# More bands of two 3x3 convolutions in the mixed form, with the statistics of their outputs taken by accumulators

## The chip, the cores and the metric

The kernel runs on one core of a Trainium2 chip, as one launch. The metric is the device time of a run in microseconds; lower is better. Five engines work side by side, each through its own queue in order: TensorE (PE) multiplies, VectorE (DVE) and ScalarE (ACT) do elementwise work, GpSimd (POOL) does small fills and issues some DMAs, SyncE (SP) issues the other DMAs. They wait for each other by semaphores.

## The reference

Two layers on x of shape (4, 128, 64, 64), fp32. The first is group norm, 4-head attention over the 4096 pixels of an image, a projection and a residual. The second is what the change is about:

```python
def conv3x3_decomposed(x, wq):
    xp = jnp.pad(x, ((0, 0), (0, 0), (1, 1), (1, 1)))
    out = jnp.zeros((B, wq.shape[0], H, W), dtype=x.dtype)
    for kh in range(3):
        for kw in range(3):
            out = out + jnp.einsum('bchw,oc->bohw', xp[:, :, kh:kh + H, kw:kw + W], wq[:, :, kh, kw])
    return out
...
residual = x
out = conv3x3_decomposed(x, lsq_quantize(w1, alpha1))
out = jax.nn.relu(batchnorm(out, gamma1, beta1))
out = conv3x3_decomposed(out, lsq_quantize(w2, alpha2))
out = batchnorm(out, gamma2, beta2)
out = jax.nn.relu(out + residual)
```

`batchnorm` takes the mean and variance of a channel over all images and pixels, so a convolution has to be finished before its normalization is known, and the second convolution cannot begin before that.

## The kernel before

Attention comes first: 32 blocks of 512 queries, in an order of the queues that is written out by hand. It leaves its result `y0` in device memory, one image of 128 x 4096 each. The change does not touch it, apart from the last of its side tasks, which load and split the first bands.

Each convolution (`layer(i, prepare, done)`) goes through 16 bands, four of 16 rows in each image. Bands are numbered m = 0 to 15, band 3 being the last of image 0; `bandlist` holds them. There are two ways to compute a band.

- Plain (`conv`, L814): the input is split into a rounded part `hi` and the remainder `lo`, and two halves of 8 rows are summed in PSUM over 9 taps and the two parts: 2 x 18 = 36 matmuls of 128x512. Evacuation: for each half, DVE takes statistics from PSUM (BN_STATS, L928), then ACT copies it to `cv` (L929).
- Mixed (`conv_by_two`, L860): rows go in pairs. DVE forms a difference of rows two apart (`vo`, L594) and the sum and difference of neighbouring rows (`vi`, L596 and L597); ACT rounds both (`uo`, `ui`, L605) and DVE takes the remainders (`lo`, `li`, L607). The four products need 3 taps times two parts each: 24 matmuls of 128x512, with `wmix` made from the weights by `mix_weights`. `rows_of_two` puts even and odd rows together: ACT copies one product to the odd rows (L868), DVE does two inner additions (L869, L870), which need the first PSUM tile, and two outer ones (L871, L872), which need the second. DVE then takes the statistics from `cv` (L919).

Which bands are mixed is `BY_TWO`, one set for each convolution. Band 15 is always plain and stands by itself at the end of `layer`; after it ten idle matmuls (`keep_warm`) bridge `batch_norm`.

PSUM has a pool `pss` of three tiles, two banks each, for plain bands and the first pair of a mixed band, and a pool `psa` of two single banks. The second pair of a mixed band lies alternately in two tiles of `psa` (named x and y) or in one tile of `pss` (named z).

Inputs are prepared two bands ahead: `prepare(m)` (`first` or `second`) stands in program order between the matmuls of band m and its evacuation, and prepares band m+2. In the first convolution it loads band m+3 from `y0` (`load_band`) and splits band m+2 (`split_band`); at m=5 `count_bad` tests a bound of the attention by a 1x1 matmul (`nbad`), which stands on PE behind band 5; at m=14 the weights of the second convolution are mixed. In the second convolution `relu_band` normalizes band m+2 on ACT (L974, L985) and prepares it in one go; `load_res` fetches the quarter images of `y0` for the residual. Band inputs share nine buffers of `kpool` (`stack_tile`); further parts of mixed bands lie in `upper`.

The end adds the residual on DVE (L1038), applies ReLU on ACT (L1039) and stores 16 quarter images from the queues of SP and ACT.

Of the kernel before, what the change touches and what calls it, by code (L numbers as in the profile page):

```python
# [16 lines left out]
F32 = mybir.dt.float32  # L17
AF = mybir.ActivationFunctionType
ALU = mybir.AluOpType
# [59 lines left out]
def _fast_body(ctx, tc, x, norm_w, norm_b, qkv_wt, qkv_b, proj_wt, proj_b,  # L79
# [144 lines left out]
    def stack_tile(name):  # L224
        return kpool.tile([P, KW], F32R, name=name, tag="k")

    def f32(t):
        return t.bitcast(F32)
# [340 lines left out]

    def split(t, name, beside=True):  # L570

        hi, lo = band_tile(f"hi{name}"), band_tile(f"lo{name}")
        if beside:
            nc.vector.tensor_copy(hi, f32(t))
        else:
            nc.scalar.copy(hi, f32(t))
        nc.vector.tensor_tensor(lo, f32(t), f32(hi), ALU.subtract)
        return hi, lo
# [6 lines left out]

    BY_TWO = (set((4, 6, 8, 10, 12, 14)), set((2, 4, 6, 8, 10, 12, 14)))

    def mixed(t, name):


        t = f32(t)
        outer, inner = (stack_tile(f"{n}{name}")[:, : BR * PW].rearrange("p (r w) -> p r w", w=PW)
                        for n in ("vo", "vi"))
        nc.vector.tensor_tensor(f32(outer), t[:, 0:BR, :], t[:, 2 : BR + 2, :], ALU.subtract)  # L594
        odd, even = t[:, 1 : BR + 1 : 2, :], t[:, 2 : BR + 2 : 2, :]
        nc.vector.tensor_tensor(f32(inner)[:, : BR // 2, :], odd, even, ALU.add)  # L596
        nc.vector.tensor_tensor(f32(inner)[:, BR // 2 :, :], even, odd, ALU.subtract)  # L597
        def part(n):
            if n == "uo":
                return stack_tile(f"{n}{name}")[:, : BR * PW].rearrange("p (r w) -> p r w", w=PW)  # L600
            return upper.tile([P, BR, PW], F32R, name=f"{n}{name}", tag="u")

        hi, lo = ([part(n + k) for k in "oi"] for n in "ul")
        for u, v in zip(hi, (outer, inner)):
            nc.scalar.copy(u, f32(v))  # L605
        for u, v, w in zip(hi, (outer, inner), lo):
            nc.vector.tensor_tensor(w, f32(v), f32(u), ALU.subtract)  # L607
        return [(o[:, 0::2, :], i[:, : BR // 2, :], i[:, BR // 2 :, :], o[:, 1::2, :])
                for o, i in (hi, lo)]

# [5 lines left out]
    def split_band(b, g):  # L616
        m = bandlist.index((b, g))
        way = mixed if m in BY_TWO[0] else lambda t, name: split(t, name, m < 3)
        ready[0, b, g] = way(raw[b, g], f"0_{b}_{g}")

# [219 lines left out]
    wq.append(mid.tile([P, TAPS, P], F32R, name="wq1"))  # L840
    upper = ctx.enter_context(tc.tile_pool(name="upper", bufs=6))
    wmix = mid.tile([P, 2, 3, P], F32R, name="wmix")
# [20 lines left out]

    def rows_of_two(a, c, y):

        even, odd = (y.rearrange("p (r e w) -> p r e w", e=2, w=W)[:, :, e, :] for e in range(2))
        a0, a1, c0, c1 = (u.rearrange("p (r w) -> p r w", w=W) for u in (*a, *c))
        nc.scalar.copy(odd, a1)  # L868
        nc.vector.tensor_tensor(even, odd, a0, ALU.add)  # L869
        nc.vector.tensor_tensor(odd, a0, odd, ALU.subtract)  # L870
        nc.vector.tensor_tensor(even, even, c0, ALU.add)  # L871
        nc.vector.tensor_tensor(odd, odd, c1, ALU.subtract)  # L872

# [25 lines left out]
    def layer(i, prepare, done):  # L899


        st = mid.tile([P, B * NB, 6], F32, name=f"st{i}")
        end = mid.tile([P, 15], F32, name=f"end{i}")
        nc.gpsimd.memset(end[:, 0:1], float((B * NB - 2) * FB))
        for m, (b, g) in enumerate(bandlist[:-1]):
            if m in BY_TWO[i]:
                a = conv_tile(i, b, g)
                a = [a[:, j, :] for j in range(2)]
                if (max(BY_TWO[i]) - m) % 4:
                    c = [psa.tile([P, FB], F32, name=f"c{i}_{b}_{g}{j}", tag="a") for j in "xy"]  # L910
                else:
                    c = pss.tile([P, 2, FB], F32, name=f"c{i}_{b}_{g}z", tag="s")
                    c = [c[:, j, :] for j in range(2)]
                conv_by_two(ready[i, b, g], a, c, i)
                prepare(m)
                y = cv[b][:, 2 * g * FB : (2 * g + 2) * FB]
                rows_of_two(a, c, y)
                for j in range(2):
                    nc.vector.bn_stats(st[:, b * NB + 2 * g + j, :], y[:, j * FB : (j + 1) * FB])  # L919
                continue  # L920
            ps = done[m] if m < len(done) else conv_tile(i, b, g)
            for j in range(2):
                if m >= len(done):
                    conv(ready[i, b, g], ps[:, j, :], j, wq[i])
            prepare(m)
            for j in range(2):
                c = 2 * g + j
                nc.vector.bn_stats(st[:, b * NB + c, :], ps[:, j, :])  # L928
                nc.scalar.copy(cv[b][:, c * FB : (c + 1) * FB], ps[:, j, :])  # L929
        nc.vector.bn_aggr(end[:, 1:3], st.rearrange("p j s -> p (j s)")[:, : 6 * B * NB - 12])  # L930
        nc.vector.tensor_scalar(end[:, 2:3], end[:, 2:3], float((B * NB - 2) * FB), None, ALU.mult)
        b, g = bandlist[-1]
        for j in range(2):
            ps = psa.tile([P, FB], F32, name=f"c{i}_last{j}", tag="a")
            conv(ready[i, b, g], ps, j, wq[i])
            c = 2 * g + j
            nc.vector.bn_stats(end[:, 3 + 6 * j : 9 + 6 * j], ps)
            nc.scalar.copy(cv[b][:, c * FB : (c + 1) * FB], ps)
        prepare(len(bandlist) - 1)
        keep_warm(10)  # L940
        return batch_norm(i, end)

    def count_bad():
# [7 lines left out]
        nc.vector.tensor_copy(cnt, nbad[0:1, 0:1])  # L951

    def first(m):
        if m == 5:
            count_bad()
        if m == 5:
            raw["w"] = f32(stack_tile("raw_w"))[:, : TAPS * P].rearrange("p (t o) -> p t o", o=P)
            nc.sync.dma_start(out=raw["w"], in_=wqd)
        if m == 6:
            nc.vector.tensor_copy(wq[1], raw["w"])  # L960
        if m == 14:
            mix_weights(1)
        if 0 < m < len(bandlist) - 3:
            load_band(*bandlist[m + 3])
        if m + 2 < len(bandlist) and m > 0:
            split_band(*bandlist[m + 2])

    a1, c1 = layer(0, first, early)

    def relu_rows(b, g, t, r0, r1):  # L970

        inner, lo, hi = t["inner"]
        a, e = max(r0 + g * BR - 1, lo), min(r1 + g * BR - 1, hi)
        nc.scalar.activation(inner[:, a - lo : e - lo, :],  # L974
                             cv[b].rearrange("p (h w) -> p h w", w=W)[:, a:e, :], AF.Relu,
                             bias=c1, scale=a1)
        nc.scalar.copy(t["hi"][:, r0:r1, :], f32(t["t"])[:, r0:r1, :])
        nc.vector.tensor_tensor(t["lo"][:, r0:r1, :], f32(t["t"])[:, r0:r1, :],
                                f32(t["hi"])[:, r0:r1, :], ALU.subtract)

    def relu_band(b, g, pieces=((0, BR + 2),)):
        if bandlist.index((b, g)) in BY_TWO[1]:
            t = band_tile(f"t1_{b}_{g}")
            inner, lo, hi = border(t, g)
            nc.scalar.activation(inner, cv[b].rearrange("p (h w) -> p h w", w=W)[:, lo:hi, :],  # L985
                                 AF.Relu, bias=c1, scale=a1)
            ready[1, b, g] = mixed(t, f"1_{b}_{g}")
            return
        t = {n: band_tile(f"{n}1_{b}_{g}") for n in ("t", "hi", "lo")}
        t["inner"] = border(t["t"], g)  # L990
        for r0, r1 in pieces:
            relu_rows(b, g, t, r0, r1)
        ready[1, b, g] = t["hi"], t["lo"]

# [13 lines left out]
    ready[1, b0, g0] = t["hi"], t["lo"]  # L1008
    relu_band(*bandlist[1])

# [4 lines left out]
    def load_res(b, i):  # L1015
        if b < B - 1:
            t = mid.tile([P, HN], F32, name=f"res{b}_{i}")
        else:
            t = f32(stack_tile(f"res{b}_{i}"))[:, :HN]
        res[b, i] = t  # L1020
        nc.sync.dma_start(out=t, in_=y0[b][:, i * HN : (i + 1) * HN])

    def second(m):
        if m + 2 < len(bandlist):
            relu_band(*bandlist[m + 2])
        if m < 4 * B - 4:
            load_res(m // 4, m % 4)

    a2, c2 = layer(1, second, [])
    for i in range(4):  # L1030
        load_res(B - 1, i)
    for b in range(B):
# [468 lines left out]
```

## Time and profile before

| what | value |
|---|---|
| median of 3 runs | 2512.17 us (2512.08 to 2512.52) |
| profiled execution, first to last instruction | 2511.1 us |
| PE busy | 2471.6 us, 98% of the span |
| DVE busy | 2194.6 us, 87% |
| ACT busy | 2123.7 us, 85% |
| statistics of the first convolution merged (`bmv`, L887) | at 2359.94 us |
| statistics of the second convolution merged | at 2481.11 us |

The three runs are times of whole executions; the profiled execution is a further one, of which the page gives the span. The profile gives each instruction of that one execution with start, duration and what it waited for. "L814" is a line of the kernel; `c<-hi,wq` is an instruction's output and inputs. In a row of groups the count, the busy time and the mean duration come first, then the idle time of the engine just before these instructions and what ended it. In a row of the timeline the start and the duration are in us, and a bracket at the end tells how long the engine had been idle and whom it waited for. A row of windows gives, for a stretch of the execution, its length, the busy time and number of instructions of each engine, the granted TensorE clock, the DMA share and the DMA rate.

### The profile page before, as it was taken

The page shows a single profiled execution, that of the slowest core. Times are in us where ns is not written, and L with a number is a line of the kernel's source. Part 1 is how long each engine was busy: PE and PEld are TensorE (multiplying, and loading weights), DVE is VectorE, ACT ScalarE, POOL GpSimd, SP SyncE. Part 2 cuts the span into 40 slices and gives each one's busy share as a digit, 9 for nine tenths or more (in the row PEclk, how much of TensorE's full clock was granted, in tenths as well). Part 3 has the DMA queues.
Part 4 walks back from the last instruction along what each step waited for, and adds up shares of the span by engine and source line. Part 5 has one row for each costly group of instructions (what it writes and reads, how often), then busy time and mean ns, then how long its engine had stood idle before and what let it go on. Part 6 is the DMA issues. An engine that isn't in the chain of part 4 may idle for free.

```text
span 2511.1 us, 64860 instructions
## 1 busy us (share of the span) xinstructions
PE 2471.6 (98%) x28552; PEld 1473.1 (59%) x28552; DVE 2194.6 (87%) x1486; ACT 2123.7 (85%) x2306; POOL 281.6 (11%) x461
## 2 busy tenths in 40 slices
PE   9999999999999999999999999999999999999995
PEld 6555555555555555555555555555555555567774
DVE  6899888899988988889988888889999999978686
ACT  5999888999988889999989889989999999954354
POOL 2111111111011111111011111110001010010000
PEclk9999999999999999999999999999999999999998
DMA  6877667788766676787757676797666666664204
GB/s 198 191 181 169 169 176 173 171 200 187 181 155 165 175 170 155 167 207 183 172 143 191 167 156 161 169 217 178 141 143 144 143 133 150 142 135 93 110 1 169
DMA packets 148954, 403.85 MB, mean 161 GB/s; under 512 B 59416, under 2 KB 60184, under 8 KB 120120
## 3 DMA queue, kind: packets, MB, share of 16 engines
q0 software_dynamic: 45840, 280.39, 48.9%
q1 hardware_dynamic: 100952, 113.60, 17.1%
q10 hardware_dynamic: 1872, 5.64, 0.6%
q8 instruction: 226, 3.70, 0.6%
q14 instruction: 64, 0.52, 0.1%
HBM read 107.48 MB, written 56.42 MB: 65 GB/s over the span
## 4 chain that ended last, share of the span: by engine, by line
PE 89%; issue 4%; DMA 3%; DVE 2%; ACT 1%; POOL 0%; ACTq 0%; SPq 0%; POOLq 0%; DVEq 0%
PE s L442 41%; PE acc L456 37%; PE c L814 3%; DMA rm<-p 3%; PE l L488 1%; PE pq L317 1%; PE c L860 1%; PE po L317 1%; PE pv L317 1%; PE pk L317 1%; DVE r L471 1%; PE c_2z L860 1%; ACT res L1039 0%; ACT p L444 0%; PE c_last L814 0%
## 5 line engine op out<-in xcount | busy, mean ns | idle before, releaser
L444 ACT ACTIVATE p<-s 128x1024 f32<-128x1024 f32 x2048 | 1950.5, 1032 | 201.9 <-PE s L442 154.0
L471 DVE TENSOR_TENSOR r<-r,p 128x2048 f32<-128x2048 f32 x768 | 1757.9, 2289 | 64.4 <-ACT p L444 14.0
L442 PE MATMUL s<-q,k 64*128 64x512 f32 x8192 | 1138.9, 409 | 2.1 <-ACT p L444 2.0
L456 PE MATMUL acc<-p,v 128*32 128x256 f32 x16384 | 1026.4, 383 | 0.0
L442 PEld LDWEIGHTS s<-q,k 64*128 64x128 f32 x8192 | 715.6, 184 | 410.9 <-issue 165.9
L456 PEld LDWEIGHTS acc<-p,v 128*32 128x32 f32 x16384 | 462.4, 109 | 483.7 <-issue 248.5
L466 POOL DMA_DIRECT2D rm<-p x160 | 139.5, 872 | 808.5 <-ACT p L444 602.0
L929 ACT COPY cv<-c 128x512 f32<-128x512 f32 x34 | 19.9, 586 | 101.6 <-DVE st L928 101.6
L352 DVE SCALAR_TENSOR_TENSOR kst<-pk,b,kst 128x512 fp32r<-128x512 f32 x32 | 24.0, 750 | 83.3 <-PE s L442 68.5
L469 DVE TENSOR_TENSOR r<-p,p 128x2048 f32<-128x2048 f32 x32 | 73.2, 2287 | 12.4 <-ACT p L444 10.7
L814 PE MATMUL c<-hi,wq 128*128 128x512 f32 x306 | 79.1, 403 | 1.6 <-ACT hi L1003 1.3
L814 PE MATMUL c<-lo,wq 128*128 128x512 f32 x306 | 78.5, 400 | 0.0
L352 DVE SCALAR_TENSOR_TENSOR qst<-pq,b,qst 128x512 fp32r<-128x512 f32 x32 | 24.0, 751 | 58.5 <-PE s L442 45.5
L814 PEld LDWEIGHTS c<-hi,wq 128*128 128x128 f32 x306 | 57.2, 188 | 19.2 <-issue 2.1
L814 PEld LDWEIGHTS c<-lo,wq 128*128 128x128 f32 x306 | 57.6, 188 | 15.4
L356 POOL DMA_DIRECT2D qd<-qst x31 | 23.6, 760 | 263.0 <-DVE qst L352 221.1
L492 POOL DMA_DIRECT2D r<-rm x31 | 26.2, 844 | 216.7 <-DMA rm<-p 86.9
L928 DVE BATCH_NORM_STATS2 st<-c 128x6 f32<-128x512 f32 x34 | 23.7, 697 | 20.8 <-ACT cv L929 11.2
L356 POOL DMA_DIRECT2D kd<-kst x27 | 20.0, 740 | 174.8 <-DVE kst L352 166.3
L464 POOL DMA_DIRECT2D rm<-p x32 | 17.8, 557 | 177.2 <-ACT p L444 100.6
L488 PE MATMUL l<-r,ones 128*32 128x256 f32 (+1 forms) x504 | 37.7, 382 | 0.0
L351 ACT ACTIVATE kst<-pk,b 128x512 fp32r<-128x512 f32 x32 | 22.3, 699 | 17.3 <-PE pk L317 17.2
(185 smaller groups left out, 1023.9 us busy)
## 6 DMA issues: line engine op xcount, KB each, us to landing
rm<-p POOLq DMA_DIRECT2D x192, 1024.0 KB, 8.0
q<-qd SPq DMA_DIRECT2D x248, 128.0 KB
r<-rm POOLq DMA_DIRECT2D x31, 1024.0 KB, 7.9
x<-in_x_dram SPq DMA_DIRECT2D x86, 256.0 KB
k<-kd SPq DMA_DIRECT2D x124, 128.0 KB
qd<-qst POOLq DMA_DIRECT2D x31, 512.0 KB, 5.1
kd<-kst POOLq DMA_DIRECT2D x27, 512.0 KB, 5.0
y<-x POOLq DMA_DIRECT2D x32, 256.0 KB, 6.4
```

What stands on the lines that cost most here:

```text
L317: nc.tensor.matmul(out[cs, :], w[:, cs], x, start=True, stop=True)
L352: nc.vector.scalar_tensor_tensor(lo, ps[what], bias, t[:, 0, :], ALU.add, ALU.subtract)
L356: (nc.sync if start else nc.gpsimd).dma_start(out=dst[b, j].rearrange("s p n -> p s n"), in_=t)
L442: nc.tensor.matmul(s[:, i, :], k[r, half, c0 : c0 + P], q[r, half, part, :], start=(part == 0), stop=(part == 1))
L444: nc.scalar.activation(pts[step][:, 2 * half : 2 * half + 2, :], s, AF.Exp, scale=SCALE)
L456: nc.tensor.matmul(acc[n][h * D : (h + 1) * D, cs], v[:, kt % KB, h * D : (h + 1) * D], pt[:, h, cs], start=(kt == 0 and half == 0), stop= ...
L466: nc.gpsimd.dma_start(out=msum[n], in_=pt, accum_op=ALU.add)
L469: nc.vector.tensor_tensor(rsum[n], pts[step - 1], pt, ALU.add)
L471: nc.vector.tensor_tensor(rsum[n], rsum[n], pt, ALU.add)
L488: nc.tensor.matmul(t["l"][h * D : (h + 1) * D, cs], ones, r[:, h, cs], start=first, stop=end)
L814: nc.tensor.matmul(ps.rearrange("p (r w) -> p r w", w=W), w[:, tap, :], part[:, r0 + kh : r0 + kh + RB, kw : kw + W], start=(n == 0), stop ...
L860: nc.tensor.matmul(ps.rearrange("p (r w) -> p r w", w=W), w[:, kw, :], part[m][:, :, kw : kw + W], start=(n == 0), stop=(n == 5))
```

## The change

`BY_TWO` grows from 6 + 7 to 9 + 10 bands, so 19 of 32 bands are mixed. `uo` moves to the pool `upper`, which gets 12 buffers instead of 6.

For mixed bands the two BN_STATS go. The two outer additions become SCALAR_TENSOR_TENSOR with an accumulator output, the sum; ACT squares the finished band of 1024 elements with an accumulator output, its bias being minus the mean of band 0 (`shift`). At the end of a layer these sums are merged with the statistics of the plain bands by six small instructions more than before.

Preparation is cut into parts. `begin` forms `vo`, `vi` and the rounded copies, `rest` the remainders, `later` does loads, the count and the ReLU. In a mixed band they are placed between the steps of evacuation: odd copy, `begin`, inner additions, `rest`, `later`, outer additions, square. In plain bands the evacuation comes after all three. In the second convolution ReLU is applied to band m+3, one band before its preparation. Mixing the weights of the second convolution moves behind the preparation of its band 1. The residual of image 2 is loaded, like that of image 3, after the second convolution in program order, into buffers of `upper`.

```diff
-    BY_TWO = (set((4, 6, 8, 10, 12, 14)), set((2, 4, 6, 8, 10, 12, 14)))
+    BY_TWO = (set((3, 4, 6, 7, 9, 10, 12, 13, 14)), set((2, 3, 4, 6, 7, 9, 10, 12, 13, 14)))
...
-    def mixed(t, name):
+    def mixed_parts(t, name):
...
+        def mix():
+            nc.vector.tensor_tensor(outer, t[:, 0:BR, :], t[:, 2 : BR + 2, :], ALU.subtract)
+            odd, even = t[:, 1 : BR + 1 : 2, :], t[:, 2 : BR + 2 : 2, :]
+            nc.vector.tensor_tensor(inner[:, : BR // 2, :], odd, even, ALU.add)
+            nc.vector.tensor_tensor(inner[:, BR // 2 :, :], even, odd, ALU.subtract)
+            for u, v in zip(hi, (outer, inner)):
+                nc.scalar.copy(u, v)
+
+        def rest():
+            for u, v, w in zip(hi, (outer, inner), lo):
+                nc.vector.tensor_tensor(w, v, f32(u), ALU.subtract)
...
-    upper = ctx.enter_context(tc.tile_pool(name="upper", bufs=6))
+    upper = ctx.enter_context(tc.tile_pool(name="upper", bufs=12))
...
-        nc.scalar.copy(odd, a1)
-        nc.vector.tensor_tensor(even, odd, a0, ALU.add)
-        nc.vector.tensor_tensor(odd, a0, odd, ALU.subtract)
-        nc.vector.tensor_tensor(even, even, c0, ALU.add)
-        nc.vector.tensor_tensor(odd, odd, c1, ALU.subtract)
+
+        def copy():
+            nc.scalar.copy(odd, a1)
+
+        def inner():
+            nc.vector.tensor_tensor(even, odd, a0, ALU.add)
+            nc.vector.tensor_tensor(odd, a0, odd, ALU.subtract)
+
+        def outer():
+            nc.vector.scalar_tensor_tensor(even, even, 1.0, c0, ALU.mult, ALU.add,
+                                           accum_out=sums[:, 0:1])
+            nc.vector.scalar_tensor_tensor(odd, odd, 1.0, c1, ALU.mult, ALU.subtract,
+                                           accum_out=sums[:, 1:2])
...
         for m, (b, g) in enumerate(bandlist[:-1]):
+            begin, rest, later = prepare(m)
             if m in BY_TWO[i]:
...
                 conv_by_two(ready[i, b, g], a, c, i)
-                prepare(m)
                 y = cv[b][:, 2 * g * FB : (2 * g + 2) * FB]
-                rows_of_two(a, c, y)
-                for j in range(2):
-                    nc.vector.bn_stats(st[:, b * NB + 2 * g + j, :], y[:, j * FB : (j + 1) * FB])
+                k = two.index(m)
+                copy, inner, outer = rows_of_two(a, c, y, sums[:, 2 * k : 2 * k + 2])
+                copy()
+                begin()
+                inner()
+                rest()
+                later()
+                outer()
+                junk = ready[i, b, g][0][4].rearrange("p r w -> p (r w)")[:, : 2 * FB]
+                nc.scalar.activation(junk, y, AF.Square, bias=shift[:, 1:2],
+                                     accum_out=squares[:, k : k + 1])
                 continue
...
-            prepare(m)
+            begin()
+            rest()
+            later()
...
+            if m == 0:
+                mv = small.tile([P, 2], F32, name=f"first{i}", tag="mv")
+                nc.vector.bn_aggr(mv, st[:, 0:2, :].rearrange("p j s -> p (j s)"))
+                nc.vector.tensor_copy(shift[:, 0:1], mv[:, 0:1])
+                nc.vector.tensor_scalar(shift[:, 1:2], mv[:, 0:1], -1.0, None, ALU.mult)
...
-        if m == 14:
-            mix_weights(1)
...
+    mix_weights(1)
+    relu_band(2)
...
     def second(m):
+        begin = rest = nothing
         if m + 2 < len(bandlist):
-            relu_band(*bandlist[m + 2])
-        if m < 4 * B - 4:
-            load_res(m // 4, m % 4)
+            begin, rest = parts_of(1, m + 2, raw[1, m + 2])
+
+        def later():
+            if m + 3 < len(bandlist):
+                relu_band(m + 3)
+            if m < 4 * B - 8:
+                load_res(m // 4, m % 4)
+
+        return begin, rest, later
```

## Prediction, made before the changed kernel was run

> **What bounds the kernel now.** I read in this order: granted clock and stages, TensorE's own order of time in the convolutions, then the groups of VectorE (DVE) and ScalarE (ACT) there. First the windows by stage: attention; its end; first convolution; second; tail.
>
> ```profile
> core 0: us, PE busy (x) PEld busy (x) DVE busy (x) ACT busy (x) POOL busy (x), PEclk, DMA share, GB/s
> 0.00:2207.00 2207.00, 2198.63 (x27178) 1266.31 (x27182) 1968.65 (x1212) 1986.36 (x2152) 270.10 (x374) 1.00 0.72 169
> 2207.00:2258.00 51.00, 51.00 (x434) 31.86 (x427) 38.97 (x32) 24.21 (x27) 4.93 (x16) 1.00 0.65 136
> 2258.00:2361.00 103.00, 101.66 (x436) 79.87 (x435) 79.82 (x113) 35.25 (x45) 2.63 (x27) 1.00 0.44 123
> 2361.00:2481.00 120.00, 118.71 (x504) 93.68 (x503) 86.85 (x110) 59.47 (x65) 3.43 (x45) 1.00 0.05 18
> 2481.00:2511.10 30.10, 1.57 (x15) 1.38 (x13) 20.31 (x23) 18.43 (x18) 0.55 (x1) 0.59 0.71 281
> ```
>
> The change lies in the third and fourth stretch. PE is full there at clock 1.00, DVE at 72 to 78%. PE waits only twice within the first convolution. Its timeline there:
>
> ```profile
> 2262.90 2.42 PE L814 MATMUL c<-hi,wq 128*128 128x512 f32 x9 [0.32 <-ACT hi L576]
> ...
> 2287.09 0.19 PE L950 MATMUL nbad<-ones,bad 128*1 128x1 f32 x2 [1.02 <-DVE bad L948]
> ```
>
> So matmuls removed here are time saved, as long as DVE and ACT can still prepare the bands. The chain that ended last gives the price: a plain band is "8.60 PE c L814 x36", so 0.239 us a matmul; a mixed band has 24, 5.74 us. What DVE and ACT need for a band (groups of the two convolutions, name, count, busy us, mean ns and idle before; then, with min/median/max ns, the tail's two instructions and the attention's last addition; last the table load):
>
> ```profile
> L928 DVE BATCH_NORM_STATS2 st<-c 128x6 f32<-128x512 f32 x34 | 23.7, 697 | 20.8 <-ACT cv L929 11.2 <-PE c L814 9.6
> L919 DVE BATCH_NORM_STATS2 st<-cv 128x6 f32<-128x512 f32 x26 | 16.7, 686 | 0.5
> L607 DVE TENSOR_TENSOR li<-vi,ui 128x1056 fp32r<-128x1056 f32 x13 | 16.4, 1258 | 0.0
> L594 DVE TENSOR_TENSOR vo<-t 128x1056 f32<-128x1056 f32 x13 | 16.3, 1251 | 11.7 <-ACT t L985 11.7
> L871 DVE TENSOR_TENSOR cv<-cv,c_0x 128x512 f32<-128x512 f32 x6 | 4.1, 676 | 0.0
> ```
>
> ```profile
> L1038 DVE SCALAR_TENSOR_TENSOR res<-cv,ba,res x17: 744/1275/1277, 2482.8 to 2500.8; 128x1024 f32<-128x1024 f32 x15, 128x512 f32<-128x512 f32 x2
> L1039 ACT ACTIVATE res<-res,bc x17: 721/1134/1149, 2483.5 to 2503.7; 128x1024 f32<-128x1024 f32 x15, 128x512 f32<-128x512 f32 x2
> ```
>
> ```profile
> L547 DVE SCALAR_TENSOR_TENSOR x<-po,bp,x x32: 742/746/751, 168.1 to 2253.9; 128x512 f32<-128x512 f32 x32
> ```
>
> ```profile
> L627 ACT ACT_TABLE_LOAD x1 | 1.3, 1283 | 2.7 <-issue 2.7
> ```
>
> Queued DVE instructions overlap by 0.08 us: vo, starting at 2266.21, is followed at 2267.37.
>
> **The change part by part.**
>
> *Matmuls.* Six more bands are mixed: 6 x 12 x 0.239 = 17.2 us less for PE, 8.6 in each convolution.
>
> *DVE per mixed band.* Preparation (L594, L596, L597, two of L607) takes 1.16 + 0.62 + 0.63 + 1.21 + 1.18 = 4.8 us and stays. The two L919 go: -1.3. The inner additions stay at 0.72 + 0.61. The outer ones (L871, L872) become SCALAR_TENSOR_TENSOR with a running sum, a form that the trace doesn't show. Bounds: 0.68, the TENSOR_TENSOR of that size, and 1.28 (below). Nearest is L547, PSUM operand and the same 512 elements, at 0.75. I take 0.75 without overlap: 0.67 to the next instruction, and half a 128x1 instruction (0.15, L948) for writing out the sum. With the wait of the second for the first, evacuation is 2.8 us, a mixed band 7.6.
>
> *Steady state.* The pattern becomes plain, mixed, mixed. PE: 8.60 + 2 x 5.74 = 20.1 us. DVE: two preparations 9.6, two mixed evacuations 5.7, one plain preparation 1.3, one plain evacuation 2.0 (with L928's wait for ACT), and 1.2 when the next mixed band's odd copy stands on ACT behind the plain band's second L929: 19.8. So PE stays the bound, by 0.3 us in 20. ACT: 2 x 1.08 + 0.58 a mixed band, and L985's 1.35 in the second convolution, and the square. Nearest row for the square: L1039, 128x1024 with a bias, 1.13; with a write-out 1.25 (bounds 1.05 and 1.5). Sum in the second convolution: 2 x 5.3 + 3.7 = 14.3 of 20.1, so it is hidden; at 1.5 it would cost 1 us, because a copy behind it comes late. A table load for Square would be 1.28 once; the trace has one load for Exp, Relu and Copy, and I take zero.
>
> *Start of the first convolution.* DVE gets there at 2259.07 in both. Band 3 was plain: PE needed one ACT cast, begun at 2261.66. Now it is mixed. After the second L928 (ends 2261.15) stand the shift's three small instructions (0.55 with their waits), then vo, vi, vi: 1.16 + 0.62 + 0.70, then ui on ACT, 1.08 with its hand-over 1.12: PE starts at 2265.3 where band 2 ended 2262.58. Then li is 0.55 late and band 1's PSUM tile 0.4: 3.6 of waiting for 0.3. Cost 3.3.
>
> *Band 4.* The PSUM pool has three tiles; band 3 takes two (its second pair is of kind z), so band 4 needs the tile of band 2. DVE does band 1's statistics (2266.6 to 2268.6), band 4's preparation (4.8, to 2273.4), and only then band 2's two L928 (2.0) and ACT's copy (0.6): 2276.0. PE ends band 3 at 2265.3 + 5.74 + 0.95 = 2272.0. Cost 4.0.
>
> *nbad.* count_bad is queued on DVE behind band 7's preparation. From 2276.4, when band 3's odd copy is there, DVE evacuates 3 and prepares 5 (4.2), evacuates 4 and prepares 6 (7.6), prepares 7 (4.8) and tests (0.4): 2293.4. PE ends bands 4 and 5 at 2276.0 + 14.3 = 2290.3. It waits 3.1 where it waited 1.0. Cost 2.1. From there DVE has caught up, and by the sums of the steady state nothing waits until the end.
>
> *Start of the second convolution.* Bands 2, 3, 4 are mixed in a row, 17.2 us for PE; evacuating them and preparing 4, 5 and 6 takes DVE 7.6 + 4.2 + 7.6 = 19.4. Band 7's tile is band 5's; it comes about 1.9 late. mix_weights(1), 2 us on DVE, moves from band 14 of the first convolution to here, behind bands 0 and 1, which are 17.2 us of PE. Cost 1.9.
>
> *At nothing:* the six small instructions of the two merged statistics (about 1.2 us) and the last square lie beside the last band's 8.6 us on PE. Activation one band ahead removes DVE's wait for L985 (11.7 us in total), which PE never felt. One more memset a layer goes to POOL, which waits for buffers anyway. Band loads are queued behind the preparation on SP, but their buffer is free two bands before. Four residual loads of 512 KB move behind the second convolution in program order, because their buffers are now `upper`'s: eight late loads, 4.2 MB, instead of four. They can go when band 12 gives its buffers back, some 25 us before the end; at the 236 to 269 GB/s that the earlier twelve got, that is 16 to 18 us, beside a DMA share of 0.05. Tail unchanged.
>
> Sum: 17.2 - 3.3 - 4.0 - 2.1 - 1.9 = 5.9 us. Walking the five queues in program order with these durations gives 6.4 (walked like this, the program of before puts the two normalizations 121.1 us apart; the trace 121.17). I take 6.2. The profiled span is 2511.1, the median 2512.17, 1.1 around it: **2506.0 us**.
>
> **Two rules against it.** L1038 reads two fp32 tensors from SBUF, 1024 elements in 1275 ns, about the pace of the plain L594 (1056 in 1251). The Trainium skill (Vector Engine (DVE) Microarchitecture Reference, Points that are easy to get wrong) says that this instruction runs at half rate with two sources that aren't bf16, as no port is left for the accumulator. The row shows no halving, but has no accumulator; here, one source is PSUM. By the row 0.75; by the rule, with (1275 - 746)/512 = 1.03 ns an element, 0.53 more: 1.28, and the sum would be 2524 (case D). I go by the row and keep the rule for the range.
>
> The granted clock was 1.00 in both convolutions, with no wait over 1.3 us. The skill (TensorE: Matmul & The Clock Gate, Part 1: The HAM clock gate) says that an idle window of about 3.4 us halves the clock. My wait at band 4 is 4.0. By the rows nothing; by the rule an estimated 3.4 us at half speed, 1.7 lost, partly given back as DVE catches up. I take zero: such a window must lie wholly in the gap.
>
> **The rivals.**
>
> A, the forecast: accumulators nearly free, PE still the bound, the starts cost 11. 2504.5 to 2507.5. For: the row sums. Against: a margin of 0.3 in 20.
>
> B, the starts cost little: PE waits of before only, the full 17.2, down to 2495; with half of the stalls, 2500.5. For: the starts are few bands, where shorter hand-overs count. Against: the PSUM tile of band 2 and ui of band 3 are real waits.
>
> C, the sum or the square costs more: DVE is the bound. Every 0.1 on the outer additions is 38 x 0.1 = 3.8, less the 2.1 of spare in six patterns. At 0.95: +5.5, 2511.5. The case spans 2507.5 to 2516.
>
> D, slower: the half rate of the rule at the outer additions. 38 x 0.53 - 2.1 = 18 against 6.2 gained: 2524. Break-even is at 0.97 an addition; slower by over 0.2% from 1.10. For: the rule and no row with a sum. Against: L1038 isn't halved.
>
> That the mixing doesn't happen is excluded: the program issues 72 fewer matmuls.
>
> **How the numbers follow.** A 0.56, B 0.11, C 0.21, D 0.12. 0.2%, about what a measurement of this kernel can tell from no change, is 5.0 us: the line is 2507.15. Faster: 0.50 of A and B, 0.61. Same: 0.06 of A and C, 0.27. Slower: D, 0.12. The range, 2500 to 2514, leaves out D, a third of B, and the top of C.
>
> **What would show it.** Right: PE's waits at band 3 (3.6), band 4 (4.0), nbad (3.1) and band 7 of the second convolution (2), nowhere else; the first convolution as long as before within 1 us, the second 6.5 shorter; the new additions at 0.68 to 0.8, squares at 1.1 to 1.3. Wrong: additions over 0.95, waits in every pattern, a granted clock under 1.00, a second table load, or residual loads inside the tail.

## The result and the profile after

The changed kernel takes 2504.35 us, median of 6 runs (2503.4 to 2506.32), where the kernel before took 2512.22 beside it: a ratio of 0.997, with a 95% interval of 0.9958 to 0.9981. That is 7.9 us less, where 6.2 were forecast. The profiled execution is one of the longer of the six: 2506.32 us with a span of 2504.6.

First the windows by stage, as they were read for the kernel before, with the borders put at the two normalizations of this run.

```profile
core 0: us, PE busy (x) PEld busy (x) DVE busy (x) ACT busy (x) POOL busy (x), PEclk, DMA share, GB/s
0.00:2207.00 2207.00, 2198.32 (x27158) 1266.51 (x27158) 1967.92 (x1212) 1985.21 (x2151) 270.11 (x374) 1.00 0.72 169
2207.00:2258.00 51.00, 51.00 (x443) 31.61 (x442) 39.35 (x30) 25.29 (x28) 4.72 (x10) 1.00 0.63 131
2258.00:2361.00 103.00, 96.32 (x394) 74.50 (x393) 84.99 (x141) 46.07 (x62) 2.57 (x32) 0.97 0.42 109
2361.00:2474.80 113.80, 111.95 (x479) 88.16 (x478) 93.72 (x151) 71.97 (x87) 3.96 (x46) 1.00 0.11 38
2474.80:2504.60 29.80, 1.46 (x14) 1.27 (x12) 20.25 (x22) 18.43 (x18) 0.55 (x1) 0.59 0.71 285
```

The second convolution is shorter; the first is not, although it has 36 matmuls less: TensorE (PE) is idle there for 6.7 us, and the granted clock has fallen to 0.97. The attention's end moves from one profile to the next (the end of band 2 lies between 2261.06 and 2265.06 in those told of here, though none of them changes TensorE's matmuls before it), so I cut the stages at events of the convolutions themselves: the end of band 2's last matmul, the first matmul of band 6 (behind nbad), and the two normalizations (bmv).

| us | before | after | difference |
|---|---|---|---|
| start to end of band 2 | 2262.58 | 2263.65 | +1.07 (nothing changed there) |
| end of band 2 to band 6 | 24.63 | 30.28 | +5.65 |
| end of band 2 to the first normalization | 97.36 | 97.40 | +0.04 |
| first to second normalization | 121.17 | 113.75 | -7.42 |
| second normalization to the end | 29.99 | 29.80 | -0.19 |

The sum is the -6.5 us of the two spans. The second convolution comes out between 113.68 and 113.80 in seven profiles that leave it as the change made it, so these differences mean something to 0.1 us, far less than what separates the runs of one kernel.

PE's timeline at the start of the first convolution is the part to compare with the one shown of before (start, duration, line, operation, count, and idle time before with its releaser):

```profile
2266.27 0.98 PE L874 MATMUL c<-ui,wmix 128*128 128x512 f32 x3 [2.62 <-ACT ui L600]
2267.57 0.99 PE L874 MATMUL c<-li,wmix 128*128 128x512 f32 x3 [0.31 <-DVE li L604]
...
2276.90 1.65 PE L874 MATMUL c<-ui,wmix 128*128 128x512 f32 x3 [3.61 <-ACT cv L970]
2278.34 1.48 PE L874 MATMUL c<-li,wmix 128*128 128x512 f32 x3
...
2282.18 0.95 PE L874 MATMUL c_0x<-uo,wq 128*128 128x512 f32 x3
...
2293.81 0.19 PE L1004 MATMUL nbad<-ones,bad 128*1 128x1 f32 x2
...
2413.37 0.98 PE L874 MATMUL c<-ui,wmix 128*128 128x512 f32 x3 [0.61 <-ACT cv L970]
```

Band 3 waits for ui and li, band 4 for the PSUM tile of band 2, band 7 of the second convolution (2413.37) for that of band 5. Beyond these there is the 1.2 us at the second convolution's first cast, which the kernel before has too, and nothing else. The forecast's wait for nbad is not there, but only just:

```profile
2293.50 0.15 DVE L1002 TENSOR_SCALAR bad<-big 128x1 f32<-128x1 f32 x1
```

Where PE waits for this instruction, nbad starts 0.2 us after its start (before: 2286.88 and 2287.09). Here it starts 0.3 us after it, at 2293.81: DVE's test was ready a mere 0.1 us before PE came. PE was late because groups of three matmuls in band 4 take 1.48 us instead of 0.88. The windows of 2 us say why: the clock is at 0.50 (column PEclk).

```profile
2274.00:2276.00 2.00, 0.00 (x0) 0.00 (x0) 1.35 (x3) 0.58 (x1) 0.00 (x0) 0.88 0.93 189
2276.00:2278.00 2.00, 1.10 (x3) 0.91 (x4) 0.86 (x2) 1.74 (x3) 0.00 (x0) 0.50 0.00 0
2278.00:2280.00 2.00, 2.00 (x6) 1.57 (x5) 1.97 (x4) 0.41 (x1) 0.00 (x0) 0.50 0.00 0
2280.00:2282.00 2.00, 2.00 (x6) 1.56 (x5) 2.00 (x6) 0.59 (x1) 0.00 (x0) 0.50 0.44 60
2282.00:2284.00 2.00, 2.00 (x9) 1.54 (x9) 2.00 (x4) 2.00 (x4) 0.19 (x3) 0.91 0.59 235
```

Band 4, from 2276.90 to the next band's start at 2285.14, takes 8.24 us instead of 5.74: 2.5 us go to the clock. The forms that no trace had shown came out as follows (outer addition of one tile pair, its write-out, the square, its write-out; min/median/max ns):

```profile
L891 DVE SCALAR_TENSOR_TENSOR cv<-cv,c_2z x4: 677/679/683, 2301.0 to 2467.1; 128x512 f32<-128x512 f32 x4
L891 DVE DVE_READ_ACCUMULATOR cv<-cv,c_2z x4: 82/84/85, 2301.6 to 2467.7; 128x1 f32 x4
...
L957 ACT ACTIVATE uo<-cv,shift x19: 1149/1152/1157, 2281.4 to 2468.5; 128x1024 fp32r<-128x1024 f32 x19
L957 ACT ACTIVATION_READ_ACCUMULATOR uo<-cv,shift x19: 183/185/188, 2282.5 to 2469.6; 128x1 f32 x19
```

The addition with a sum takes no longer than the plain one of the same size (0.69 us, L887). The timeline has what comes behind them:

```profile
2287.28 0.68 DVE L891 SCALAR_TENSOR_TENSOR cv<-cv,c_0x 128x512 f32<-128x512 f32 x1
2287.89 0.08 DVE L891 DVE_READ_ACCUMULATOR cv<-cv,c_0x 128x1 f32 x1
2287.89 0.68 DVE L893 SCALAR_TENSOR_TENSOR cv<-cv,c_0y 128x512 f32<-128x512 f32 x1
```

```profile
2392.97 1.15 ACT L957 ACTIVATE uo<-cv,shift 128x1024 fp32r<-128x1024 f32 x1 [2.54 <-DVE cv L893]
2394.03 0.18 ACT L957 ACTIVATION_READ_ACCUMULATOR uo<-cv,shift 128x1 f32 x1
2394.12 0.56 ACT L884 COPY cv<-c 128x512 f32<-128x512 f32 x1
```

The next addition starts 0.61 us after the first, and the next copy 1.15 us after the square: each write-out overlaps with what follows. There is one table load in the profile, as before. The residual loads run at 235 GB/s from 2450 to 2460 us and the DMA queues are empty from 2470, ahead of the tail.

### The profile page after: what moved, and what is told of

Read it like the earlier page. It is cut to its first block, busy times and chain, and to the rows that moved or that the text cites. A ratio compares the mean times of both kernels' runs of the same rounds, so it can differ in the third digit from the quotient of the medians.

```text
span 2504.6 us, 64822 instructions
## 1 busy us (share of the span) xinstructions
PE 2459.0 (98%) x28480; PEld 1462.1 (58%) x28480; DVE 2206.2 (88%) x1552; ACT 2147.0 (86%) x2344; POOL 281.9 (11%) x463
## 3 DMA queue, kind: packets, MB, share of 16 engines
q1 hardware_dynamic: 100952, 113.60, 17.2%
## 5 line engine op out<-in xcount | busy, mean ns | idle before, releaser
L466 POOL DMA_DIRECT2D rm<-p x160 | 139.1, 869 | 799.4 <-ACT p L444 556.8
L957 ACT ACTIVATE uo<-cv,shift 128x1024 fp32r<-128x1024 f32 x19 | 21.9, 1153 | 53.1 <-DVE cv L893 50.5
L828 PE MATMUL c<-hi,wq 128*128 128x512 f32 x198 | 51.2, 403 | 1.2 <-ACT hi L1045 1.2
L828 PE MATMUL c<-lo,wq 128*128 128x512 f32 x198 | 50.8, 401 | 0.0
L970 ACT COPY cv<-c 128x512 f32<-128x512 f32 x22 | 12.9, 586 | 38.4 <-DVE st L969 38.4
L828 PEld LDWEIGHTS c<-hi,wq 128*128 128x128 f32 x198 | 36.9, 188 | 13.1 <-issue 2.1
L828 PEld LDWEIGHTS c<-lo,wq 128*128 128x128 f32 x198 | 37.3, 188 | 10.0
L874 PE MATMUL c<-ui,wmix 128*128 128x512 f32 x114 | 35.2, 418 | 6.8 <-ACT cv L970 4.2
```

The lines of the kernel that those rows point to most:

```text
L466: nc.gpsimd.dma_start(out=msum[n], in_=pt, accum_op=ALU.add)
L828: nc.tensor.matmul(ps.rearrange("p (r w) -> p r w", w=W), w[:, tap, :], part[:, r0 + kh : r0 + kh + RB, kw : kw + W], start=(n == 0), stop ...
L874: nc.tensor.matmul(ps.rearrange("p (r w) -> p r w", w=W), w[:, kw, :], part[m][:, :, kw : kw + W], start=(n == 0), stop=(n == 5))
```

## The experiments

Two questions. First, which part of the change carries the 7.4 us of the second convolution: the number of mixed bands, the accumulators, or the order? Second, where did the first convolution's 8.6 us go: to three waits that each cost what they show, or to one chain on VectorE (DVE) that sets band 6, whatever PE does before? Theory 1 is the chain; the rival is the waits with the slow clock. For the second question the stage times of one profile are more exact than the medians, whose intervals are 2 to 3 us to either side in most of these runs, and I go by them. All runs in one table (stages in us, from the profile of each):

| kernel | mixed bands | median | ratio to before, interval | end of band 2 to band 6 | first conv. | second conv. |
|---|---|---|---|---|---|---|
| before | 13 | 2512.22 | | 24.63 | 97.36 | 121.17 |
| after | 19 | 2504.35 | 0.997 (0.9958 to 0.9981) | 30.28 | 97.40 | 113.75 |
| old statistics | 19 | 2515.12 | 1.0011 (1.0005 to 1.0018) | 32.27 | 100.72 | 118.37 |
| 13 bands | 13 | 2516.69 | 1.0018 (1.0011 to 1.0024) | 27.12 | 101.40 | 121.12 |
| old order | 19 | 2510.84 | 0.9992 (0.9986 to 0.9999) | 30.85 | 97.95 | 118.70 |
| activation late | 19 | 2530.97 | 1.0067 (1.0053 to 1.008) | 30.19 | 97.32 | 138.86 |
| 24 fillers | 19 | 2505.58 | 0.9973 (0.9964 to 0.9982) | 30.19 | 97.30 | 113.78 |
| test early | 19 | 2505.07 | 0.9971 (0.996 to 0.9981) | 29.47 | 96.52 | 113.68 |
| test early, 24 fillers | 19 | 2505.27 | 0.997 (0.9959 to 0.9981) | 30.47 | 97.50 | 113.69 |
| fillers in both waits | 19 | 2506.42 | 0.9974 (0.9962 to 0.9985) | 30.17 | 98.75 | 113.80 |
| test early, both fillers | 19 | 2502.78 | 0.9958 (0.9944 to 0.9972) | 28.16 | 95.14 | 113.69 |
| band 3 plain | 18 | 2505.07 | 0.9966 (0.9954 to 0.9978) | 28.08 | 97.34 | 113.78 |
| three edits of order | 18 | 2499.05 | 0.9944 (0.9931 to 0.9958) | 23.58 | 92.10 | 112.81 |

### What carries the second convolution

**Old statistics.** The outer additions become plain, and each mixed band gets its two bn_stats back.

```
-            nc.vector.scalar_tensor_tensor(even, even, 1.0, c0, ALU.mult, ALU.add,
-                                           accum_out=sums[:, 0:1])
-            nc.vector.scalar_tensor_tensor(odd, odd, 1.0, c1, ALU.mult, ALU.subtract,
-                                           accum_out=sums[:, 1:2])
+            nc.vector.tensor_tensor(even, even, c0, ALU.add)
+            nc.vector.tensor_tensor(odd, odd, c1, ALU.subtract)
...
-                nc.scalar.activation(junk, y, AF.Square, bias=shift[:, 1:2],
-                                     accum_out=squares[:, k : k + 1])
+                for j in range(2):
+                    nc.vector.bn_stats(st[:, 2 * m + j, :], y[:, j * FB : (j + 1) * FB])
```

> The changed kernel with the old statistics: 19 mixed bands and the interleaved order stay, the outer additions are plain again, each mixed band gets two bn_stats on VectorE instead of the running sums and ScalarE's square. Theory 1, VectorE's room is what carries the change: 1.2 to 1.3 us more on VectorE for a mixed band put a plain-mixed-mixed period at about 22.3 us against TensorE's 20.1, so VectorE falls behind in every second or third band; TensorE's wait for nbad grows to about 5 us, new waits of 1.6 to 2.6 us appear in both convolutions, the first is about 3 us longer than in the changed kernel (97.4 us from the end of band 2 to the normalization), the second 4 to 5 (113.8); total 2511 to 2514, that is no gain over the kernel before. Rival, the accumulators are a convenience and the number of mixed bands does it alone: 2503 to 2506.

Measured: 2515.12, slower than before by 0.11% (0.05 to 0.18), with 72 matmuls less than before. The waits of PE in the two convolutions (total, times, longest):

```profile
PE c L874 <- ACT cv L966: 8.8, 5, 2.6
PE nbad L988 <- DVE bad L986: 3.3, 1, 3.3
```

Waits for the PSUM tile of a plain band now stand at five places: band 4 and band 13 of the first convolution, bands 7, 10 and 13 of the second. Three of them are behind the starts, where the changed kernel has none. Only the nbad wait fell short of the 5 us expected, and the total came out 1 us above the expected range. In sum, more mixed bands without the accumulators bring nothing: the second convolution keeps 2.8 us of what it gained over the kernel before, and the first loses 3.4.

**13 bands.** The reverse: accumulators, order and early activation with the old sets of bands.

```
-    BY_TWO = (set((3, 4, 6, 7, 9, 10, 12, 13, 14)), set((2, 3, 4, 6, 7, 9, 10, 12, 13, 14)))
+    BY_TWO = (set((4, 6, 8, 10, 12, 14)), set((2, 4, 6, 8, 10, 12, 14)))
```

> The changed kernel with the 13 mixed bands of before (4, 6, 8, 10, 12, 14 and 2, 4, 6, 8, 10, 12, 14): accumulators, interleaved order and early activation alone. Theory 1, TensorE is the bound, and room on VectorE buys nothing by itself: the second convolution takes 121 us as in the kernel before (121.2), the first 97.4 plus what the later place of the nbad test costs, 3 to 4 us of wait where the kernel before waited 1.0, so 99.5 to 101; total 2512 to 2515. Rival, the cheaper evacuation alone brings the time down: 2505 to 2508.

Measured: 2516.69, slower than before by 0.18% (0.11 to 0.24). The second convolution, 121.12, is that of before (121.17). The first is 4.0 longer (101.40, expected 99.5 to 101): the wait for nbad is 3.5 us instead of 1.0, and the band behind it has the clock at half, which the expectation left out. Room on DVE buys nothing where PE is the bound; the gain takes the number and the accumulators together.

**Old order.** In the mixed bands the whole preparation stands ahead of the evacuation again.

```
-                copy()
                 begin()
-                inner()
                 rest()
                 later()
+                copy()
+                inner()
                 outer()
```

> The changed kernel with the order of before in the mixed bands: the whole preparation of the band two ahead first, and only then the odd copy, the inner and the outer additions. 19 mixed bands and accumulators stay. Theory 1, VectorE has only 0.3 us to spare in a period of 20.1: with the odd copy queued on ScalarE behind the casts of the preparation, VectorE waits for ScalarE in each mixed band; the first convolution 0.5 to 1 us longer than in the changed kernel (97.4), the second 5 to 7 us longer (113.8), where ScalarE has the activation besides, with waits of TensorE of 1 to 2.5 us at bands 7, 10 and 13; total 2510 to 2512. Rival, the order is of no account, since VectorE has the same work: 2504 to 2505.

Measured: first convolution +0.55, second +4.95, total 2510.84, as theory 1 had it, but not by the waits it named. PE waits 1.8 us at band 7 and only 0.4 and 0.3 at bands 10 and 13; 0.7 at band 5 and 1.0 at the last band come to it. And I had put DVE's wait at the odd copy of each mixed band. DVE's waits in the second convolution (this kernel):

```profile
DVE lo L617 <- ACT hi L614: 10.1, 5, 2.4
DVE cv L887 <- ACT cv L884: 4.9, 9, 1.8
```

and in the changed kernel:

```profile
DVE cv L887 <- ACT cv L884: 7.7, 5, 1.8
...
DVE lo L617 <- ACT hi L614: 1.8, 1, 1.8
```

The wait stands at the preparation of the plain band: DVE has nothing between a cast that ScalarE (ACT) has just begun and the subtraction that reads it. The interleaved order puts the inner additions there.

**Activation late.** The activation of the second convolution goes back in front of the preparation that reads it.

```
-    relu_band(2)
...
         if m + 2 < len(bandlist):
+            relu_band(m + 2)
             begin, rest = parts_of(1, m + 2, raw[1, m + 2])
...
-            if m + 3 < len(bandlist):
-                relu_band(m + 3)
```

> The changed kernel with the activation of the second convolution where it was before: ahead of the preparation of the same band, not a band earlier. All else stays. Theory 1: VectorE waits for the activation (1.3 us and the hand-over, behind ScalarE's square of 1.3) at the begin of each preparation; in the kernel before these 11.7 us were free, for VectorE had 28% to spare, now they are on the path. The first convolution stays at 97.4 us, the second becomes 20 to 27 us longer than 113.8, with waits of TensorE at every period of three bands; total 2524 to 2531. Rival, the waits are taken up by the slack that is left, as the prediction had them cost nothing: 2504 to 2508.

Measured: the second convolution is 25.1 us longer, total 2530.97. DVE's largest waits there:

```profile
DVE vo L595 <- ACT t L1033: 21.2, 9, 2.7
DVE cv L887 <- ACT cv L884: 12.5, 5, 3.0
```

Before, DVE waited 11.7 us for this activation and PE felt none of it. Here the wait costs the whole gain and 18.8 us more. It is free only while DVE has room. The expectation left out the clock, though. The second convolution here, to be compared with the fourth row of the windows above (length, then PE busy; the clock stands third from the end):

```profile
2362.38:2501.24 138.86, 121.50 (x479) 93.82 (x478) 94.52 (x150) 72.63 (x87) 3.99 (x46) 0.93 0.09 31
```

For the same matmuls PE is idle 15.5 us longer and busy 9.6 us longer: well over a third of the 25 us is half clock behind the new waits, the longest of them 6.0 us. That the total fell into the expected range is in part luck.

### Where the first convolution's part went

**24 fillers.** Matmuls of no use in the wait ahead of band 4, to keep the clock up.

```
                 conv_by_two(ready[i, b, g], a, c, i)
+                if i == 0 and m == 3:
+                    keep_warm(24)
```

> The changed kernel with 24 small matmuls of no use (about 2.9 us) queued on TensorE between band 3 and band 4 of the first convolution, where it waits 3.6 us; nothing else differs. If the half clock from 2275 to 2282 us follows from that wait, the granted clock is 1.00 through band 4 and its 24 matmuls take 5.8 us instead of 8.2. Theory 1, the start is a chain of VectorE up to the test for nbad, and the slow clock lies beside it: TensorE then waits about 2.4 us for nbad, where it waited for nothing, band 6 starts as late as before within 0.3 us, total 2504 to 2505. Rival, the slow clock is on the path: the first convolution is 2.4 us shorter, total 2502.

Measured: inconclusive. Fillers took 5.5 us (48 passes in the trace) and overran the wait. Band 4 ran at full clock, but band 3 had half the clock behind its own wait of 2.62 us, which had left it at 1.00 in the profile shown above. Band 6 came 30.19 us after band 2, as without fillers.

**Test early.** DVE's part of the test for nbad moves from behind band 7's preparation to behind band 3's.

```
+    def sum_bad():
...
+            if m == 1:
+                count_bad()
             if m == 5:
-                count_bad()
+                sum_bad()
```

> The changed kernel with VectorE's two instructions of the test (the maximum and the comparison) moved from behind the preparation of band 7 to behind that of band 3; the nbad matmul and the copy of its sum stay where they are. Theory 1: TensorE no longer has to wait for VectorE at nbad, but it arrives there late anyhow, because of the slow clock in band 4: band 6 starts only 0 to 0.5 us earlier (its li is ready at about the same time as nbad was, but its first matmuls need only ui, 1.3 us earlier), total 2503.5 to 2504.5. Rival, the test's place costs what the prediction gave it: 2 us shorter, total 2502.3.

Measured: 0.81 us sooner at band 6 and 0.88 in the first convolution, against the 0 to 0.5 of theory 1 and the 2 of the rival. In this profile band 4's slow clock lasted half as long: it fell back to 0.98 us a group after two groups of 1.65 and 1.48; band 3 began at half clock as well. The median, 2505.07, shows no gain over the changed kernel. Together with the 24 fillers:

> Both of the last two edits: the test early, and 24 small matmuls in the wait before band 4. Theory 1, the slow clock and the late test cover each other: only together do they bring the time down, by 2.3 to 2.6 us in the first convolution, total about 2501.9. Rival, each counts by itself and adds up: one of the two runs before has already shown its own part, and this one shows the sum. If neither matters (another chain of VectorE holds band 6), it stays at 2504.

30.47 us and 97.50: no gain, because the fillers overran the wait again and band 3 was slowed before them. This run tells nothing of the chain.

**Fillers in both waits,** sized to end inside them (10 calls behind band 2, 13 behind band 3).

> The changed kernel with small matmuls of no use in both waits of the start of the first convolution: 10 calls ahead of band 3, where TensorE waits 2.6 us, and 13 ahead of band 4 (3.6 us). One call came out as 0.23 us in the run with 24 calls, 5.5 us in all, which overran the wait by 1.9 us; now they take 2.3 and 3.0 us and end inside. If the half clock comes from these waits, the granted clock is 1.00 from 2258 us on. Theory 1, the start is a chain of VectorE up to the test for nbad: TensorE reaches nbad 2.4 us earlier than in the changed kernel and waits there for 2 to 2.8 us; from the end of band 2 to band 6 it is 30.0 to 30.3 us as in the changed kernel (30.28); the first convolution stays at 97.4 us, total 2504 to 2505. Rival, the slow clock is on the path: both 2.4 us shorter, total 2502.

Measured, PE's timeline of this run:

```profile
2264.55 0.98 PE L874 MATMUL c<-ui,wmix 128*128 128x512 f32 x3 [0.39 <-ACT ui L600]
...
2275.18 0.99 PE L874 MATMUL c<-ui,wmix 128*128 128x512 f32 x3 [0.71 <-ACT cv L974]
...
2291.98 0.19 PE L1008 MATMUL nbad<-ones,bad 128*1 128x1 f32 x2 [2.21 <-DVE bad L1006]
2292.10 0.99 PE L874 MATMUL c<-ui,wmix 128*128 128x512 f32 x3
2292.93 1.19 PE L874 MATMUL c<-li,wmix 128*128 128x512 f32 x3
2293.92 1.48 PE L874 MATMUL c<-ui,wmix 128*128 128x512 f32 x3
```

Bands 3 to 5 have the full clock, PE is at nbad 2.2 us earlier, waits there, and band 6 starts 30.17 us after band 2 (30.28). So it is DVE's chain that sets band 6, and the slow clock ahead of it costs nothing of its own: the rival is out. What I had not expected is the end: 2.2 us of waiting bring the half clock back behind nbad, where no wait covers it, and the first convolution grows by 1.35 us.

The run with the activation late shows the same without a filler, for its first convolution has the same instructions as that of the changed kernel:

```profile
2267.69 1.65 PE L874 MATMUL c<-ui,wmix 128*128 128x512 f32 x3 [2.62 <-ACT ui L600]
...
2278.31 1.00 PE L874 MATMUL c<-ui,wmix 128*128 128x512 f32 x3 [1.90 <-ACT cv L970]
...
2295.13 0.19 PE L1004 MATMUL nbad<-ones,bad 128*1 128x1 f32 x2 [2.22 <-DVE bad L1002]
2295.25 0.99 PE L874 MATMUL c<-ui,wmix 128*128 128x512 f32 x3
```

There the half clock fell on band 3 and band 4 ran at full clock. PE waited 2.2 us for nbad, where the forecast had its wait, and the clock stayed at 1.00 behind it. Band 6 came after 30.19 us and the first convolution took 97.32, within 0.1 of the changed kernel's own profile. So whether the wait for nbad shows depends on where the clock falls, and the sum does not.

**Test early, with these fillers.**

> The same small matmuls, and VectorE's part of the test for nbad behind the preparation of band 3 instead of band 7. With the early test alone, the trace gave 29.5 us from the end of band 2 to band 6 and 96.5 us for the first convolution, with 3.3 us of half clock in band 4. Theory 1, slow clock and late test cover each other: no wait for nbad and full clock, 27.6 to 28.0 us to band 6, the first convolution 94.8 to 95.2 us, total 2501.5 to 2502.5. Rival, band 6 waits for another part of VectorE's chain (its ui or li): 29.5 us and 96.5 us again, total 2503.5.

```profile
2275.95 1.00 PE L874 MATMUL c<-ui,wmix 128*128 128x512 f32 x3 [0.70 <-ACT cv L974]
...
2290.48 0.19 PE L1012 MATMUL nbad<-ones,bad 128*1 128x1 f32 x2
2290.60 0.98 PE L874 MATMUL c<-ui,wmix 128*128 128x512 f32 x3
```

28.16 us to band 6 (0.2 above the range expected) and 95.14 for the first convolution, median 2502.78. The slow clock and the late test had covered each other: each edit alone brought at most 0.9 us, both 2.3.

**Band 3 plain.** It drops out of the first set; PE has 12 matmuls more.

> The changed kernel with band 3 of the first convolution plain, so 18 mixed bands: TensorE has 12 matmuls (2.9 us) more, VectorE some 4 us less in the start. Theory 1, the start is bound by VectorE: the waits at band 3 and band 4 go (0.4 us is left), TensorE reaches nbad early and waits there 4 to 5 us, band 6 starts 2 to 2.3 us earlier than in the changed kernel (28.0 to 28.3 us after the end of band 2 instead of 30.28), and the first convolution takes 95.1 to 95.4 us; if the clock is halved behind that wait, up to 2 us of it come back in bands 6 and 7. Total 2502 to 2504. Rival, a mixed band less is a loss of 2.9 us, since the starts cost what they cost: 2507.

```profile
2290.69 0.19 PE L1004 MATMUL nbad<-ones,bad 128*1 128x1 f32 x2 [4.44 <-DVE bad L1002]
2290.81 1.65 PE L874 MATMUL c<-ui,wmix 128*128 128x512 f32 x3
2292.25 1.48 PE L874 MATMUL c<-li,wmix 128*128 128x512 f32 x3
```

The waits at bands 3 and 4 are gone but for 0.3 us, and band 6 starts 28.08 us after band 2, 2.2 us sooner, with 2.9 us more of matmuls. The half clock behind the 4.4 us wait takes the 2.2 back: 97.34. In the first convolution a mixed band less costs nothing.

**Three edits of order.** Band 3 plain, the test early, and in the second convolution never three mixed bands in a row while a band is still to be prepared.

```
+    BY_TWO = (set((4, 6, 7, 9, 10, 12, 13, 14)), set((2, 3, 5, 6, 8, 9, 11, 12, 13, 14)))
```

> Three edits of order together: band 3 of the first convolution plain, the test for nbad early, and in the second convolution bands 2, 3, 5, 6, 8, 9, 11, 12, 13, 14 mixed (ten as before, but never three in a row ahead of a band still to be prepared). 18 mixed bands. Theory 1, at these starts the gain went lost: waits of TensorE of 0.4 us at band 3 and about 1.5 us at band 7 of the first convolution, none in the second; no half clock; first convolution about 92.0 us (97.4 in the changed kernel), second about 112.5 us (113.8); total 2497.5 to 2499. Rival, only the number of mixed bands counts: 2507. Rival, half of the way: the waits move to bands behind (band 7 or 10), 2501.

Measured: 2499.05 us, ratio 0.9944 (0.9931 to 0.9958), 13.8 us under the kernel before beside it. All waits of PE in the two convolutions:

```profile
PE c L828 <- ACT hi L1052: 1.2, 1, 1.2
PE c L874 <- ACT cv L970: 1.1, 1, 1.1
PE c L828 <- ACT hi L614: 0.3, 1, 0.3
```

The clock is at 1.00 in both. The stages came out as expected within 0.3 us. With 18 mixed bands this version is 5.3 us faster by the medians than the change with 19; the stages say 5.3 in the first convolution and 0.9 in the second. The two intervals touch (0.9958), so it is the stages that carry this. What each of the three edits brings here was not taken apart, except that only the new set of bands touches the second convolution.

## Why the prediction was right, point by point

- **Sum and price.** 72 matmuls at 0.239 us, 17.2 us, with 11 us of it lost at the starts: 2506.0 forecast, 2504.35 measured. By the stages 9.8 of the 17.2 were lost. The first convolution was to stay as long as before within 1 us (+0.04), the second to be 6.5 shorter (7.42).
- **DVE per mixed band.** The row-based 0.75 us for the outer addition was a little high: 0.68 and a hidden write-out, 0.61 us from one instruction to the next. Both together take 1.21 us where the forecast had 1.47. The steady state holds: no wait of PE in it. (The spare of 2.1 us in six patterns is 1.8 by the forecast's own 0.3; no case hangs on it.) Old statistics and old order show how narrow that is.
- **The half-rate rule.** One fp32 source from SBUF and one from PSUM with a running sum are not halved: 0.68 us against 0.69 for the plain addition. Case D is out. The Trainium skill (Vector Engine (DVE) Microarchitecture Reference, Points that are easy to get wrong) speaks of two sources in SBUF, so this does not contradict it; the forecast had stretched the rule to a case that it does not name. Two SBUF sources with a sum were not tried.
- **Square.** 1.15 and 0.19 for the write-out, which overlaps with the next instruction; 1.25 was taken for both. It is hidden, as forecast, and there is no second table load.
- **Start of the first convolution.** Waits of 2.6 and 0.3 (3.6 forecast) and 3.6 (4.0), in their places. The step that failed is nbad: not 3.1 us but none, because of the one I had put at zero, the clock. I had weighed the rule (TensorE: Matmul & The Clock Gate, Part 1: The HAM clock gate) and found 1.7 us; it was 2.5, and it made PE so late that DVE's test was ready, by 0.1 us. In the run with the activation late, where band 4 had the full clock, PE did wait there, 2.2 us. The sum stood because DVE sets the start of band 6: its test ends 30.8 us after band 2 in my queue of times (2293.4), and band 6 came after 30.28. I had the chain, but booked it as four costs of PE that add up; they do not, as the fillers showed. That the sum would stand with a wrong term in it was not foreseen.
- **Start of the second convolution.** 1.9 us forecast at band 7, 0.6 measured. With that the second convolution gained 0.9 us more than forecast; the first, for which the terms added up to 0.8 us more than before, gained the rest.
- **At nothing.** The late residual loads and the merged statistics are hidden, and the tail is the same (29.80 and 29.99). Activation one band ahead was costed at nothing by the waits of before; that held for the kernel before, but in this one taking it back costs 25 us, 9.6 of them by the clock, and the forecast didn't say so.

## What to carry to other kernels

When one engine is relieved until a second is within 2% of it, price what the second does at every start, not only per period: there it works through a queue, and the first engine's waits are one debt, not several. Look for what stands late in that queue without need (a two-instruction test here), and try one unit less of the improvement: 18 bands without waits beat 19 with them. A wait that is free because an engine has slack stops being free when the slack is spent.

## What the runs showed of the hardware

The forecast had taken a wait of 4.0 us for safe. In the convolutions of these runs the granted clock fell to half after much shorter ones: after 2.2 us in the run with fillers in both waits, after 2.1 us and 0.3 more in the one with the old statistics, and after as little as 0.4 and 1.3 us in the one with the activation late, where the clock is at 0.50 from 2398 us:

```profile
2394.42 0.95 PE L874 MATMUL c<-ui,wmix 128*128 128x512 f32 x3 [0.41 <-DVE cv L888]
2396.66 1.57 PE L874 MATMUL c<-li,wmix 128*128 128x512 f32 x3 [1.29 <-DVE li L604]
```

Other waits left it at 1.00: 2.6 us at band 3 in the changed kernel's profile, which halved it at the same place with 24 fillers alone and with the test early alone, and 3.3 us for nbad with the old statistics. All five waits of 3.5 us and more halved it. An episode lasted about 3.4 us, or twice that as in band 4 above. The Trainium skill (page and section as above) says that the window is free-running and asks for an idle window of about 3.4 us. The free run fits the differences between executions. That the window must lie wholly in the gap, as the forecast took it, does not fit the shorter waits.

Small matmuls in the gap kept the clock at 1.00 behind them; where they ended before the data came, they did not delay PE.
